# Depthwise filter matrices on 112 partitions, loaded by four transfers of 28 partitions each

## The chip, the cores and the metric

The kernel runs on one core of a Trainium2 chip. The metric is device time in microseconds (us) of one launch; less is better. Before the change, the median of three runs is 3448.89 us (3437.99 to 3469.41).

## The reference

Input `x` is 32 images of 384 channels, 28 x 28 pixels, all float32. Two layers follow each other.

```python
# layer 0: ConvNeXt block
y = conv(x, dw_w, padding 3, groups=384) + dw_b      # 7x7 depthwise
y = layernorm_over_channels(y) * ln_g + ln_b
y = gelu(einsum('bhwc,cf->bhwf', y, w1) + b1)        # 384 -> 1536
gx = sqrt(sum(y*y, axis=(h, w)))
y = grn_g * (y * gx / (mean_f(gx) + 1e-6)) + grn_b + y
x = x + einsum('bhwf,fc->bhwc', y, w2) + b2          # 1536 -> 384
# layer 1: gate
avg, mx, mn = mean, max, min of x over (h, w)
logits = concat(avg @ W1.T, grouped(mx, W2_1) * W2_2, mn @ W3.T) @ Wfc.T
out = sigmoid(logits[:, :, None, None] + x)
```

## The kernel before

The kernel has two stages. The first is the depthwise convolution of all images, channel by channel; the second takes image after image through the two channel matrix products (`up` and `down`), with a fast matrix scheme that needs sums of weight blocks. Those sums (`form_w`) are made by ScalarE and GpSimd during the first stage and stored in device memory (`u1d`, `u2d`). The change is in the first stage.

**How the convolution is tiled.** An image has 28 rows of 28 pixels. Four rows, 112 pixels, lie on 112 partitions (`RW = 4`, `HW = 28`, `KP = 112`), and the seven groups of four rows times 32 images are the 224 columns. For one channel, the convolution is a product with a banded matrix whose row for a pixel is the same sequence of filter taps, shifted. This sequence `fs` (355 values per channel, `FL`) is written once to device memory. The filter matrix of a channel is read out of it by a transfer whose source pattern overlaps itself: the partition for pixel row r and column w starts `r * PW + w` values further on (`PW = 32`). `load_t(s)` (L420 to L432) loads the matrices of eight channels (`TC = 8`) into one of four buffers `tmat`: each of 112 partitions gets 8 x 355 values, 11,360 bytes in one piece. Step 0 is loaded in two parts of four channels.

**A step.** There are 48 steps (`NK`), of eight channels each. A step has four calls of `conv`, two channels each. `conv` issues, per channel, three matrix products (L671, L673, L675; each float32 product shows as two MATMUL records) into a PSUM tile `pc`. VectorE then transposes `pc` into `yt` (L678) and adds it to the channel sum `acc` (L686), ScalarE squares it (L692), and GpSimd sums the squares (L698). At the end of a step, ScalarE's queue stores `yt` to device memory (`yd`, L837) and then the weight sums that are ready (L853). `yt` has two buffers, the weight sums `u` four.

**The images.** A block of 32 channels of all images comes as eight loads of `x` (L456, 392 KB each, into `room` and `xi_last`), is turned by TensorE (L477), and copied into `xt` by VectorE (L484) and ScalarE (L486). The turns of the next block are spread over the four steps of this one.

**Order.** Filters, `x` and weights are loaded from SyncE's queue (SP in the profile), in program order: at the start of step s, the filters of step s + 3 (L425); then weights or constants, if any (L785); then one x load after each turned block. A filter buffer is free when the step that used it last is through TensorE. The program gives transfers eight completion counters, in turn. `hold` (L601) makes the first filter loads wait for an x load.

The last two steps are done in two halves of 16 images, so that the statistics of the first half can be finished early; the loads of the first image and `first_image` follow.

Of the kernel before, what the change touches and what calls it, by code (L numbers as in the profile page):

```python
# [13 lines left out]
P = 128  # L14
# [4 lines left out]
HW = 28  # L19
# [10 lines left out]
RW = 4  # L30
NJ = HW // RW
PW = P // RW
KP = RW * HW
XC = 32
TC = 8
# [10 lines left out]
FL = S0 + SN  # L46
# [152 lines left out]
def convnext_gate_kernel(  # L199
# [13 lines left out]
    nc = tc.nc  # L213
# [149 lines left out]
    with ExitStack() as one:  # L363
# [40 lines left out]
        NT2 = 4  # L404
        tmat = [tp.tile([KP, TC, FL], F32, name=f"tmat_{i}") for i in range(NT2)]
# [15 lines left out]
        def load_t(s, parts=1):  # L421
            base = fs[s * TC // P]
            n = TC // parts
            for i in range(parts):
                nc.sync.dma_start(  # L425
                    tmat[s % NT2][:, i * n : (i + 1) * n, :].rearrange("p c m -> p (c m)"),
                    bass.AP(
                        tensor=base.tensor,
                        offset=base.offset + (s * TC % P + i * n) * FL,
                        ap=[[PW, RW], [1, HW], [1, n * FL]],  # L430
                    ),
                )  # L432


        NX = C // XC
# [170 lines left out]
        for i in range(NG):  # L606
            if i == 0:
                load_t(0, 2)
                nc.sync.dma_start(dwb, cvec[0:1, :].broadcast_to([P, C]))
            if i == NG - 2:  # L610
                for cb in range(CB):
                    if cb:
                        keep(sequences(cb))
                    keep(nc.scalar.dma_start(fs[cb][P:, :], zrow))
            if i == NG - 2:

                hold(tmat[1][:, 0, :1], i)
                load_t(1)
            for h in range(2):
                turn_x(i, h, xt, (nc.vector, nc.scalar)[h])  # L620
            load_next(i)
# [149 lines left out]
        for s in range(NK):  # L771
            k, si = divmod(s, SK)
            if s + 3 < NK:
                if s == 0:
                    for i in range(2, 4):
                        hold(tmat[i][:, 0, :1], NG)
                        if i == 2:
                            load_t(i)
                load_t(s + 3)
# [11 lines left out]
            if s == NK - 1:  # L791
# [6 lines left out]
                for half, (b0, b1) in enumerate(((0, B0), (B0, B))):  # L798
# [7 lines left out]
                    for n in range(2 * PAIRS):  # L806
                        i, c2 = divmod(n, PAIRS)
# [16 lines left out]
            elif s < NK - 2:  # L824
                for c2 in range(PAIRS):
# [5 lines left out]
                    elif q in (2 * PAIRS + 2, 2 * PAIRS + 5, 2 * PAIRS + 8):  # L831
                        n = FB + 4 * ((q - 2 * PAIRS) // 3)
# [455 lines left out]
```

## Time and profile before

| What | Value |
|---|---|
| Median of three runs | 3448.89 us |
| The profiled execution's own time | 3448.96 us |
| Its span in the profile | 3446.9 us |
| TensorE busy in the span | 3090.9 us (90%) |
| GpSimd / VectorE / ScalarE busy | 2432.2 / 1990.0 / 1736.7 us |
| Mean granted TensorE clock | 0.944 of full speed |
| First and last full-batch filter product (L671) | 30.7 and 880.3 us |
| Filter loads | 47 of 1242.5 KB, 2 of 621.2 KB |

The table of slices divides the span into 40 parts of 86 us; a digit is the busy share of an engine in tenths. DMA is the mean over the core's sixteen DMA engines, so a transfer that uses a few of them shows as a small share. "chain" is the sequence of work and waits, followed back from the last instruction. In the view by windows, a row is a stretch of time, the columns are the busy time of each engine, then granted clock, DMA share and GB/s. Lines of waits read: who waited, for what, us in total, how often, the longest.

### The profile page before, as it was taken

The numbers are of one execution on the slowest core, as the hardware profiler recorded it, in microseconds if no ns is written. First come the engines' busy times: TensorE is split into PE (matmuls) and PEld (weight loads), VectorE is DVE, ScalarE is ACT, GpSimd is POOL, SyncE is SP. The second block draws the span as 40 slices with busy tenths as digits, with TensorE's granted clock in tenths as the row PEclk, the third lists the DMA queues.
The fourth block names the chain that finished last, engine by engine and source line by source line (L and its number), as shares of the span: only waits on it lengthen the run. The fifth ranks groups of instructions, "written<-read, shape, count | busy, mean of one in ns | idle before, by whom it ended". The sixth has DMA issues, their size and how long they took to land.

```text
span 3446.9 us, 43986 instructions
## 1 busy us (share of the span) xinstructions
PE 3090.9 (90%) x14435; PEld 2498.4 (72%) x14435; DVE 1990.0 (58%) x4554; ACT 1736.7 (50%) x2916; POOL 2432.2 (71%) x1822
## 2 busy tenths in 40 slices
PE   6586665666799999999999999999999999999998
PEld 5476565565567777777778877777778887777788
DVE  2233232333666666666666666666666666666666
ACT  1122221222365666666655665666665666566662
POOL 1222244443579888887888888888888888888887
PEclk8778787778899999999999999999999999999999
DMA  5645555554645665655666666655666666655546
GB/s 181 190 172 181 182 202 182 187 179 162 214 130 179 219 204 192 195 192 193 206 199 200 211 216 204 193 194 190 194 207 201 200 214 208 209 193 190 190 156 197
DMA packets 287167, 664.51 MB, mean 193 GB/s; under 512 B 30675, under 2 KB 111086, under 8 KB 281678
## 3 DMA queue, kind: packets, MB, share of 16 engines
q1 hardware_dynamic: 253832, 569.28, 51.2%
q10 hardware_dynamic: 33110, 92.42, 7.0%
q8 instruction: 118, 1.93, 0.2%
q14 instruction: 107, 0.88, 0.1%
HBM read 566.85 MB, written 94.76 MB: 192 GB/s over the span
## 4 chain that ended last, share of the span: by engine, by line
PE 68%; DMA 22%; POOL 4%; DVE 3%; issue 1%; ACT 1%; SPq 0%; ACTq 0%; DVEq 0%; POOLq 0%
PE ph_C L941 12%; DMA tmat<-fs 11%; PE ph_A L941 10%; PE ph_B L941 10%; PE pz_A L1071 7%; PE pz_C L1071 7%; PE pz_F L1071 6%; PE pz_D L1071 6%; DMA room<-in_x 4%; PE pz_H L1071 2%; DMA u1d<-u 2%; PE pz_I L1071 2%; PE pz_E L1071 2%; POOL d_room L1032 1%; DVE room L316 1%; DMA ws<-in_w 1%
## 5 line engine op out<-in xcount | busy, mean ns | idle before, releaser
L327 ACT ACTIVATE y<-y,fv,gsc 128x784 f32<-128x784 f32 x372 | 359.1, 1030 | 464.5 <-DVE gsc L979 464.5
L1032 POOL TENSOR_TENSOR d_room<-y 128x588 f32<-128x588 f32 x253 | 364.4, 1441 | 289.0 <-PE pz_B L1071 192.2
L941 PE MATMUL ph_C<-room,ws 128*128 128x392 f32 x1240 | 462.4, 495 | 5.4 <-DVE y L956 2.9
L941 PE MATMUL ph_B<-room,ws 128*128 128x392 f32 x1240 | 460.2, 494 | 5.4 <-DVE room L359 5.4
L941 PE MATMUL ph_A<-room,ws 128*128 128x392 f32 x1240 | 459.0, 493 | 2.1 <-ACT te L948 1.7
L900 ACT ACTIVATE y<-y,b1f 128x784 f32<-128x784 f32 x384 | 350.3, 945 | 209.1 <-DVE y L958 179.0
L1032 POOL TENSOR_TENSOR d_room<-d_room,y 128x588 f32<-128x588 f32 x308 | 440.9, 1436 | 16.8
L671 PE MATMUL pc<-xt,tmat 112*128 112x224 f32 x736 | 236.4, 407 | 198.0 <-ACT sq L692 128.1
L678 DVE STREAM_TRANSPOSE yt<-pc 128x448 f32<-128x448 f32 x184 | 118.9, 646 | 473.9 <-PE pc L675 315.9
L941 PEld LDWEIGHTS ph_C<-room,ws 128*128 128x128 f32 x1240 | 233.7, 190 | 188.6 <-DVE y L956 28.7
L698 POOL TENSOR_TENSOR ssum<-ssum,sq 128x896 f32<-128x896 f32 (+1 forms) x100 | 200.7, 2007 | 235.7 <-ACT sq L692 233.6
L941 PEld LDWEIGHTS ph_A<-room,ws 128*128 128x128 f32 x1240 | 235.7, 190 | 175.1 <-ACT te L948 2.4
L941 PEld LDWEIGHTS ph_B<-room,ws 128*128 128x128 f32 x1240 | 235.5, 191 | 169.6 <-issue 5.8
L692 ACT ACTIVATE sq<-pc,dwb 128x224 f32<-128x224 f32 x368 | 141.4, 453 | 395.9 <-DVE acc L686 262.1
L913 ACT ACTIVATE junk<-y 128x784 f32<-128x784 f32 x384 | 329.0, 857 | 8.9
L1032 POOL TENSOR_TENSOR d_room<-y,d_room 128x588 f32<-128x588 f32 x214 | 306.1, 1436 | 27.2 <-PE pz_D L1071 15.8
L359 POOL TENSOR_TENSOR room<-room 128x392 f32<-128x392 f32 x303 | 303.5, 1018 | 11.9
L671 PEld LDWEIGHTS pc<-xt,tmat 112*128 112x128 f32 x736 | 143.0, 222 | 204.5 <-ACT sq L692 131.8
L1032 POOL TENSOR_TENSOR y<-y 128x588 f32<-128x588 f32 x180 | 258.8, 1438 | 7.1
L952 DVE TENSOR_TENSOR y<-y,ph_C 128x392 f32<-128x392 f32 x384 | 212.8, 562 | 24.9
L954 DVE TENSOR_TENSOR y<-y,ph_B 128x392 f32<-128x392 f32 x256 | 137.5, 557 | 153.0 <-ACT y L900 123.4
L673 PE MATMUL pc<-xt,tmat 112*96 112x192 f32 x736 | 205.2, 365 | 0.0
(261 smaller groups left out, 6443.0 us busy)
## 6 DMA issues: line engine op xcount, KB each, us to landing
u<-u2d SPq DMA_DIRECT2D x487, 384.0 KB
ws<-u1d SPq DMA_DIRECT2D x384, 320.0 KB
tmat<-fs SPq DMA_DIRECT2D x47, 1242.5 KB
ws<-u2d SPq DMA_DIRECT2D x121, 384.0 KB
yi<-yd SPq DMA_DIRECT2D x95, 448.0 KB
yd<-yt ACTq DMA_DIRECT2D x46, 896.0 KB
x<-in_x SPq DMA_DIRECT2D x32, 1176.0 KB
out<-x ACTq DMA_DIRECT2D x31, 1176.0 KB
```

The lines of the kernel that those rows point to most:

```text
L327: eng.activation(out, in_, AF.Identity, bias=add, scale=mul)
L359: tc.keep_in_program_order(eng.tensor_tensor(d, o[in0], o[in1], op))
L671: keep(nc.tensor.matmul(po, t[:, c, P : 2 * P], xc, start=True, stop=False))
L673: nc.tensor.matmul(lo, t[:, c, 2 * P : T0 + MW], after, start=False, stop=False)
L692: nc.scalar.activation(part(sq)[:, cy % SQ + ci], part(pc[:, :, :N])[:, ci], AF.Square, bias=dwb[:, cc + ci : cc + ci + 1], scale=1.0,)
L698: nc.gpsimd.tensor_tensor(part(ssum), part(ssum), part(sq), ALU.add)
L900: ins = nc.scalar.activation(y, y, AF.Gelu, bias=b1f[:, f : f + 1], scale=1.0)
L913: ins = nc.scalar.activation(junk, ys[b][:, f, :], AF.Square, accum_out=ssqs[b][:, f : f + 1])
L941: nc.tensor.matmul(banks[t, bk][:, :NH], wts[t][:, i % UG, :], o[opnd], start=(first == 1), stop=True, skip_group_check=True,)
L952: nc.vector.tensor_tensor(d, d, p, ALU.add)
L1032: nc.gpsimd.tensor_tensor(d[0], o[a][0], o[c][0], ALU.add if sign == "+" else ALU.subtract)
L1071: nc.tensor.matmul(pz[:, :NQ4], wt[:, i % UD, t, :], o[opnd][0][:, t, :], start=(first and t == 0), stop=(t == KD - 1), skip_group_check=True,
```

## The change

Each filter load becomes four transfers, one for each of the four pixel rows. A transfer writes 28 partitions, and its source pattern has 28 starting places one value apart, instead of 4 times 28. The bytes, their places, the buffers, and the order of everything else in the source are the same. The first load, which came in two parts, becomes eight transfers.

```diff
             for i in range(parts):
-                nc.sync.dma_start(
-                    tmat[s % NT2][:, i * n : (i + 1) * n, :].rearrange("p c m -> p (c m)"),
-                    bass.AP(
-                        tensor=base.tensor,
-                        offset=base.offset + (s * TC % P + i * n) * FL,
-                        ap=[[PW, RW], [1, HW], [1, n * FL]],
-                    ),
-                )
+                for r in range(RW):
+                    nc.sync.dma_start(
+                        tmat[s % NT2][r * HW : (r + 1) * HW, i * n : (i + 1) * n, :].rearrange(
+                            "p c m -> p (c m)"
+                        ),
+                        bass.AP(
+                            tensor=base.tensor,
+                            offset=base.offset + (s * TC % P + i * n) * FL + r * PW,
+                            ap=[[1, HW], [1, n * FL]],
+                        ),
+                    )
```

## The prediction, before the result was known

> **What bounds the kernel now.** I read the page first, for where the engines are not full.
>
> ```profile
> span 3446.9 us, 43986 instructions
> ...
> PE   6586665666799999999999999999999999999998
> ...
> PEclk8778787778899999999999999999999999999999
> DMA  5645555554645665655666666655666666655546
> ...
> PE 68%; DMA 22%; POOL 4%; DVE 3%; issue 1%; ACT 1%; SPq 0%; ACTq 0%; DVEq 0%; POOLq 0%
> PE ph_C L941 12%; DMA tmat<-fs 11%; PE ph_A L941 10%; PE ph_B L941 10%; PE pz_A L1071 7%; PE pz_C L1071 7%; PE pz_F L1071 6%; PE pz_D L1071 6%; DMA room<-in_x 4%; PE pz_H L1071 2%; DMA u1d<-u 2%; PE pz_I L1071 2%; PE pz_E L1071 2%; POOL d_room L1032 1%; DVE room L316 1%; DMA ws<-in_w 1%
> ```
>
> PE is full from slice 11 on; only the first ten or so slices (86 us each) have gaps, and a lower clock. DMA holds 22% of the chain, half of it the filter loads. So only the depthwise-convolution stage matters here. The filter line dates it, and the view by windows (columns as named; last three: granted PE clock, busy share of the 16 DMA engines, GB/s) shows its resources.
>
> ```profile
> L671 PE MATMUL pc<-xt,tmat x736: 351/353/743, 30.7 to 880.3; 112*128 112x224 f32 x184
> ```
>
> ```profile
> core 0: us, PE busy (x) PEld busy (x) DVE busy (x) ACT busy (x) POOL busy (x), PEclk, DMA share, GB/s
> 30.70:903.00 872.30, 572.36 (x3113) 535.29 (x3114) 284.48 (x513) 191.29 (x509) 299.33 (x209) 0.80 0.52 181
> 84.50:88.50 4.00, 4.00 (x27) 3.85 (x25) 0.00 (x0) 0.00 (x0) 0.00 (x0) 1.00 0.26 108
> 270.00:271.00 1.00, 1.00 (x9) 0.95 (x7) 0.78 (x2) 0.28 (x1) 1.00 (x1) 1.00 0.92 378
> 900.20:902.20 2.00, 2.00 (x21) 2.00 (x21) 1.93 (x3) 0.40 (x2) 1.14 (x1) 1.00 0.99 115
> ```
>
> No engine is full over the stage, DMA least of all at 0.52. The short windows say why it still binds. At 84.5 us only filter loads are in flight: share 0.26, 108 GB/s. That is four of sixteen engines, 27 GB/s each. The load's source pattern has 4 as its outermost count; the x loads, with 32 outermost, reach share 0.92 and 378 GB/s at 270 us (25.7 GB/s per engine).
>
> Work per engine in the stage, from the table of DMA issues: filters 47 x 1242.5 KB and 2 x 621.2 KB are 61.1 MB; over four engines at 27 GB/s that is 565 us. The rest (x 96 x 392 KB, yd 46 x 896 KB and 16 x 112 KB, u1d 15 x 256 KB, u2d 38 x 192 KB, weights 6 x 768 KB) is 98.7 MB; over sixteen at 25.7 that is 240 us. The four busy engines carry 805 us of a stage of 872. They are the bound, at 92%. The waits agree:
>
> ```profile
> SPq L456 <- DMA tmat<-fs: 242.2, 19, 17.8
> ```
>
> The x loads need nothing of the filters; they wait because the program gives eight completion counters out in turn, so that each transfer waits for the one eight before.
>
> **The change part by part.**
>
> *Added issues.* 49 transfers become 196. One costs SP 0.655 us (median of L425), so 147 x 0.655 = 96 us more on SP. A step (eight channels, one load) then has 4 x 0.655 for filters and 2 x 0.54 for x, 3.7 us of 10 or more: hidden behind PE and the transfers. Uncovered it would be 96 us. Behind these issues on SP stand the x loads, which run four steps ahead; the filters run three ahead.
>
> *The engines of one load.* 28 rows dealt to up to 16 engines leave two rows on the busiest, as 14 engines with two each would. At 27 GB/s each that is 378 GB/s, 3.4 us for a load's 1.27 MB, where four engines need 11.8 us. This is the good bound.
>
> *The rate of few partitions.* The window at 900.2 us has stores of 16 partitions alone: all engines busy (0.99), yet 115 GB/s instead of 378/0.92 = 411. Few partitions slow the engines that serve them. Scaled to 28 partitions it is 115 x 28/16 = 201 GB/s, and four quarters in a row take 6.3 us. Unscaled, 115 GB/s gives 11.1 us, the bad bound. I take 6.3, since 28 is nearer to 16 than to 128 and the slowdown followed the partition count there.
>
> [...]
>
> *The step after.* The other bytes cost 240/48 = 5.0 us of every engine per step. The busiest engine then has 3.4 + 5.0 = 8.4 us (good), 6.3 + 5.0 = 11.3 us (taken), 11.1 + 5.0 = 16.1 us (bad). The other limit is PE: in a stretch without stalls, at full clock, a step's first filter matmuls start at 263.08 and the next step's at 272.85, 9.8 us. DVE, ACT and POOL had 284, 191 and 299 us in the stage, 4 to 6.2 us per step, and follow. So DMA stays the bound by a little. Before, the stage ran 872/805 = 1.08 over its DMA work; I keep that: 12.2 us per step.
>
> *The counters.* About 8.4 transfers per step through eight counters: a step can't be shorter than 1.05 times the mean time from issue to landing. With 6 to 10 us for a landing it is covered by the step; what is late first if not is the yt store, whose two buffers leave it one step (DVE's yt L678 waits 125.7 us for it now).
>
> *The start.* ACT's turn of the last x block before the first convolution waits 16.1 us for the first filter load, behind a store that shares its counter. That load shrinks from 11.8 to 6.3 us or less: first convolution at about 24 instead of 30.7 us.
>
> *The sum.* 46 whole steps, then two half-batch steps from 880 to 903 us (23 us, with filters loaded before). 24 + 46 x 12.2 + 23 = 608 us for the end of the convolutions, against 903: 295 us gained. What follows (statistics, first images, the PE-bound rest) is untouched: the same instructions behind the same waits. The profiled execution took 3448.96 us (span 3446.9 and 2.1 outside), the median of the runs is 3448.89, so one serves for both: 3449 - 295 = 3154 us.
>
> **The rivals.**
>
> *PE takes over.* If quarters and other traffic interleave so that engines rarely meet on the same partitions, DMA needs 8.4 us and PE's 9.8 rules: 46 x 9.8 = 451, end at 24 + 451 + 23 = 498, 405 us gained, 3044 us; with the same 1.08 over, 10.6 us per step, 3081. For it: x loads and stores do mix in between. Against: 9.8 and 8.4 lie close, and each stall brings PE's clock down for some 4 us (0.50 from 284 to 288 us, 0.99 in the next window).
>
> *Few partitions cost the full price.* 115 GB/s: 16.1 x 1.08 = 17.4 us, end at 847, 56 us gained, 3393 us; halfway to the taken value 14.8 us, 3273. For it: the row is the only measured one. Against: 28 rows touch more than 16 do.
>
> *No gain.* If the four quarters ran strictly one after the other and each took a quarter of the present 11.8 us, nothing moves: 3449 us. It needs 108 GB/s for 28 partitions where 16 had 115. [...]
>
> *Slower: the counters decide.* If a 28-row transfer still ran on only the same four engines, eight counters would hold two filter loads instead of eight, and x loads and stores would queue behind quarters. The point is a mean landing of 18.5/1.05 = 17.6 us, the present step being (880.3 - 30.7)/46 = 18.5. The chain of waits has pieces of filter loads of 31 to 45 us now. At a mean of 20 us a step takes 21 us: 46 x 21 = 966, end at 1020 with the old start, 117 us lost, 3566 us.
>
> **How the numbers follow.** DMA bound at the taken price, 3100 to 3230 us: 0.52, the likeliest, 3154. PE bound, 3040 to 3100: 0.24. Full price of few partitions, 3230 to 3410: 0.15. No gain: 0.03. Slower: 0.06. The range 3050 to 3290 reaches into both neighbours and leaves out under 2 in 10. A change of 1% (34 us) is about what these runs can tell from none: faster 0.91, within it 0.03, slower 0.06.
>
> **What would show it.** Right: the first convolution near 24 us, the last near 608; DMA share over the stage 0.75 or more at 260 GB/s or so; no windows left with share 0.26; the wait of L456 for filter loads under 60 us; the same work after the stage at the same length. PE bound: share below 0.7 when no transfer is awaited, clock near 0.95. Wrong: filter loads still alone at 108 GB/s (engines not added), or high share at under 200 GB/s with steps of 16 us (partitions), or SP and ACT waiting on counters while the share is low.

## The result, and the profile after

The changed kernel takes 3223.04 us in the median of four runs (3199.34 to 3234.14), the kernel before 3443.44 us beside it (four runs, 3436.96 to 3469.41). The ratio is 0.934, with a 95% interval of 0.926 to 0.941. The forecast was 3154 us.

The profiled execution of the changed kernel is its fastest run: 3199.34 us, span 3197.5. Against the profiled execution before (span 3446.9) that is 249.4 us less, where the medians differ by 220. The reading below goes by the pair of profiles. From the page of the changed kernel (the span cut into 40 slices, now of 80 us; then the chain of work that ended last):

```profile
span 3197.5 us, 44190 instructions
...
PE   7698878889999999999999999999999999999998
...
PEclk9798988999999999999999999999999999999999
DMA  8879988875566666666566666666665666666645
...
PE 81%; DMA 8%; POOL 4%; DVE 4%; issue 1%; ACT 1%; SPq 1%; ACTq 0%; DVEq 0%; POOLq 0%
```

The row of DMA reads 7 to 9 in the first eight slices, where it read 4 to 6, and DMA's share of the chain fell from 22% to 8%. PE still has gaps, in eight slices instead of eleven. The filter line dates the stage, and the view by windows (busy time of each engine, then granted TensorE clock, busy share of the DMA engines, GB/s) shows its resources:

```profile
L674 PE MATMUL pc<-xt,tmat x736: 350/353/742, 18.6 to 637.6; 112*128 112x224 f32 x184
```

```profile
core 0: us, PE busy (x) PEld busy (x) DVE busy (x) ACT busy (x) POOL busy (x), PEclk, DMA share, GB/s
18.60:658.60 640.00, 536.54 (x3110) 507.31 (x3111) 290.66 (x517) 200.54 (x511) 299.90 (x209) 0.89 0.88 248
636.20:638.20 2.00, 2.00 (x14) 1.95 (x13) 1.40 (x3) 0.71 (x3) 1.52 (x1) 1.00 1.02 217
```

The stage from the first full-batch filter product to the last half-batch one shrinks from 872 to 640 us, at a DMA share of 0.88 instead of 0.52. The second row is a window in which almost only filter quarters are in flight: at a share of 1.02 they move 217 GB/s. The trace has 14 packets in flight there for most of the time, where with filter loads alone before (from 84.5 us) it has 4. With the earlier start, the convolutions end at 659 instead of 903 us. That is 244 of the 249 us; what follows takes 2538.5 instead of 2543.9 us.

The waits on SyncE's queue changed their kind:

```profile
SPq L426 <- DMA yd<-yt: 273.8, 31, 14.1
SPq L426 <- DMA tmat<-fs: 79.5, 51, 5.4
...
SPq L459 <- DMA tmat<-fs: 9.2, 6, 3.0
```

The x loads (now L459) wait for filter loads 9 us instead of 242. In their place the issues of filter quarters (now L426) wait 274 us for the stores of `yt`, in 31 long pieces. TensorE itself waits for filter loads 83 us, where it waited 30 us before:

```profile
PE pc L674 <- DMA tmat<-fs: 82.8, 25, 7.4
```

The chain of waits between 30 and 650 us (start, length, what) shows why some quarters are late. Eleven times a store on ScalarE's queue stands in it right before filter quarters, nine times of weight sums and twice of `yt`, 91 us of stores in all. One of them:

```profile
543.49 7.86 DMA u2d<-u
551.36 5.56 DMA tmat<-fs
```

A filter load needs nothing of such a store; by the program, only the completion counters that are given out in turn link the two.

### The profile page after: what moved, and what is told of

It is laid out like the page before. It is cut to its first block, busy times and chain, and to the rows that moved or that the text cites. A ratio compares the mean times of both kernels' runs of the same rounds, so it can differ in the third digit from the quotient of the medians.

```text
span 3197.5 us, 44190 instructions
## 1 busy us (share of the span) xinstructions
PE 3048.9 (95%) x14435; PEld 2465.1 (77%) x14435; DVE 1992.8 (62%) x4554; ACT 1745.3 (55%) x2916; POOL 2433.0 (76%) x1822
## 4 chain that ended last, share of the span: by engine, by line
PE 81%; DMA 8%; POOL 4%; DVE 4%; issue 1%; ACT 1%; SPq 1%; ACTq 0%; DVEq 0%; POOLq 0%
PE ph_C L944 13%; PE ph_A L944 11%; PE ph_B L944 11%; PE pz_A L1074 7%; PE pz_C L1074 7%; PE pz_F L1074 6%; PE pz_D L1074 6%; DMA tmat<-fs 4%; PE pc L674 3%; PE pc L676 3%; PE pc L678 3%; PE pz_H L1074 2%; PE pz_I L1074 2%; PE pz_E L1074 2%; DMA u2d<-u 2%; PE pt L480 1%
## 5 line engine op out<-in xcount | busy, mean ns | idle before, releaser
L327 ACT ACTIVATE y<-y,fv,gsc 128x784 f32<-128x784 f32 x372 | 359.1, 1030 | 463.6 <-DVE gsc L982 463.6
L674 PE MATMUL pc<-xt,tmat 112*128 112x224 f32 x736 | 222.2, 386 | 91.8 <-DMA tmat<-fs 82.8
L674 PEld LDWEIGHTS pc<-xt,tmat 112*128 112x128 f32 x736 | 133.5, 208 | 99.0 <-issue 70.8
L1074 PE MATMUL pz_A<-d_room,u 128*128 128x196 f32 x1050 | 202.8, 329 | 0.1
```

The costliest lines, as they stand in the source:

```text
L327: eng.activation(out, in_, AF.Identity, bias=add, scale=mul)
L674: keep(nc.tensor.matmul(po, t[:, c, P : 2 * P], xc, start=True, stop=False))
L1074: nc.tensor.matmul(pz[:, :NQ4], wt[:, i % UD, t, :], o[opnd][0][:, t, :], start=(first and t == 0), stop=(t == KD - 1), skip_group_check=True,
```

## The experiments

A *step* below is the time from the first to the last full-batch filter product, divided by 46: 18.5 us before, 13.5 us after. Three theories were to be told apart. *A*: the DMA engines are the bound; what matters is how many engines one load uses, and the rate at which few partitions take data. *B* and *C*: the number of transfers matters, since eight completion counters let only eight be under way; the quarters use them up, and so the loads look less far ahead. The diffs show the main lines of each edit.

### More transfers without more engines: bychannel

The kernel before, with each load cut by channels instead of by rows. All the parts keep the old source pattern.

```diff
-                load_t(s + 3)
+                load_t(s + 3, 4)
```

> As before, with the pattern that uses four engines, but each filter load split into four transfers of two channels each, all on 112 partitions. It adds the transfers of the change without its engines. Theory A: the same four engines carry the same bytes, 3430 to 3480 us, as before. Theory B (counters; the prediction's slower rival): the eight counters hold two loads instead of eight, x loads and stores queue behind them, 3500 to 3570 us.

It took 3464.0 us, ratio 1.004 (1.0015 to 1.007), step 18.8 us. As many transfers as the change has, but 4 rows outermost as before, cost 0.4% and gain nothing. The window over most of its stage is nearly that of before (0.52 and 181 GB/s from 60 to 860 us):

```profile
60.00:860.00 800.00, 504.62 (x2674) 470.55 (x2672) 248.15 (x437) 159.43 (x433) 259.06 (x177) 0.78 0.52 177
```

So the gain doesn't come from shorter transfers, and the crowding of the counters costs little where the engines are the bound.

### More engines without more transfers: single

One transfer again, with the two counts of the source pattern exchanged, so that 28 is outermost. The pixels land in another order on the partitions of `tmat`, while those of `xt` stay where they are, so other pixels are convolved.

```diff
-                        ap=[[PW, RW], [1, HW], [1, n * FL]],
+                        ap=[[1, HW], [PW, RW], [1, n * FL]],
```

> One transfer per filter load as before, but with 28 as the outermost count of its source pattern (pixel column outermost, pixel row inner), so that it should use 14 engines over all 112 partitions. (The pixels of xt are left where they were, as in spread; the times stay.) Theory A: close to spread, 3080 to 3140 us; a little slower if neighbouring engines meet on the same partitions. Theory B, counters: 49 transfers instead of 196, so that the wait of SP's filter line for yt stores falls under 60 us, and faster than after as well, 3060 to 3120 us. So single alone does not separate them; if spread stays at after's time and single gains, it is the counters. If the outermost count does not set the engines, 3440 us as before.

It took 3121.2 us, ratio 0.904 (0.898 to 0.909), step 11.6 us:

```profile
60.00:530.00 470.00, 423.57 (x2558) 404.73 (x2557) 238.75 (x422) 162.40 (x423) 255.49 (x175) 0.94 0.93 290
```

The same bytes in the same number of transfers as before gain 9.6%; only the outermost count of the source differs. Filter loads alone had a share of 0.26 before, four packets in flight, and the stage's share rises from 0.52 to 0.93 here: the engine count of one load was the bound. It also gains 100 us more than the change does: with loads that spread over 112 partitions the stage moves 290 GB/s at a share of 0.93, where with quarters on 28 partitions it moved 248 at 0.88. How much of that is the partitions, the next run shows.

### The same four transfers, spread over all partitions: spread

Transfer r writes partitions r, r + 4, and so on (other pixels again, as in *single*).

```diff
-                        tmat[s % NT2][r * HW : (r + 1) * HW, i * n : (i + 1) * n, :].rearrange(
+                        tmat[s % NT2][r::RW, i * n : (i + 1) * n, :].rearrange(
```

> As after, with four transfers of 28 rows per filter load in the same order, but transfer r writes partitions r, r+4, r+8 ... instead of 28 neighbours, so each spans all 112 partitions. (The pixels of xt are left where they were, so the convolution mixes other pixels; shapes, counts and times of the work stay.) Theory A, few neighbouring partitions slow the engines that serve them: in after a filter row of 11,360 bytes runs at half rate; spread, it returns to nearly full rate, the filters cost an engine about 3.5 us of a step instead of 6, PE becomes the bound at 9.8 to 11 us a step instead of 13.5, the last convolution starts near 520 to 560 us instead of 658, and the time is 3080 to 3130 us. Theory B, the eight completion counters hold the filter transfers up (SP's filter line waits 274 us for yt stores in after): counts and order are the same, so the step stays at 13.5 us and the time at 3200 to 3235 us.

It took 3164.3 us, ratio 0.918 (0.912 to 0.924), step 12.7 us, between the two forecasts. The window and the first wait of SyncE's queue:

```profile
60.00:570.00 510.00, 435.32 (x2542) 412.69 (x2541) 239.93 (x415) 165.09 (x418) 252.37 (x173) 0.92 0.80 263
```

```profile
SPq L426 <- DMA yd<-yt: 252.6, 32, 14.0
```

More bytes (263 GB/s) at a lower share (0.80): per unit of share 263/0.80 = 329 GB/s, against 248/0.88 = 282 after the change. So the rate of 28 neighbouring partitions does cost engine time. But the step fell by 0.8 us only, and the engines are no longer full: most of what remains is not the partitions' rate. The queue waits nearly as long for `yt` stores as after the change (253 and 274 us), and TensorE still waits for filter loads, where in *single* it waits 0.7 us:

```profile
PE pc L674 <- DMA tmat<-fs: 64.6, 27, 5.6
```

In the chain between 60 and 570 us, stores of `yt` hold 21.7%, mostly with a filter quarter right behind; in *single* (60 to 530 us) they hold 5.0%. So both theories have a part here: the partitions' rate, and loads that are issued late, behind a store (the counter as the link is read from the program, not tested).

### Fewer partitions still: sixteen

The quarters of the changed kernel are cut once more, into 16 and 12 rows.

```diff
+                    for w0, w1 in ((0, 16), (16, HW)):
```

> As after, but each 28-row transfer split into one of 16 and one of 12 rows, eight transfers per load; 16 and 12 engines then serve 16 and 12 partitions. Theory A with the prediction's law (rate follows the number of neighbouring partitions, 115 GB/s at 16): a filter row takes about four times 426 ns, some 1500 ns or more, a load 11 to 13 us, the step 16 to 19 us, 3340 to 3470 us. If engines counted and partitions did not: as after or better, 3150 to 3220 us. Theory C alone: as the run eight, 3218 us.

One run: 3466.5 us, beside 3449.2 for the kernel before; step 18.5 us. The whole stage, and a window with almost only filter loads:

```profile
60.00:860.00 800.00, 539.87 (x2744) 502.46 (x2744) 257.93 (x448) 179.49 (x454) 271.44 (x185) 0.79 0.85 179
871.40:873.40 2.00, 2.00 (x13) 1.95 (x13) 1.34 (x4) 0.78 (x2) 0.72 (x1) 1.00 1.13 91
```

The whole gain is gone, at a DMA share of 0.85. How many engines served the parts of 12 rows, no view shows. This is the price of few partitions at its plainest: filter loads alone get 217 GB/s on 28 partitions and 91 on 16 and 12. It also doubles the number of transfers, which the next run does by itself.

### Twice the transfers, same partitions: eight

Every load of the changed kernel is cut by channels into two parts, so it has eight transfers of 28 partitions.

```diff
-                load_t(s + 3)
+                load_t(s + 3, 2)
```

> As after, but every filter load in two parts of four channels, so eight transfers of 28 partitions with half the bytes each. Theory A (rate of few partitions): same bytes through the same engines and partitions, step 13.5 to 14 us, 3210 to 3250 us. Theory B (counters): 12.4 transfers per step instead of 8.4 through eight counters, step up to 13.5 x 12.4/8.4 = 19.9 us, 3350 to 3520 us.

It took 3218.0 us, ratio 0.932 (0.927 to 0.937), step 13.4 us: no change against 3223. Eight transfers fill all counters by themselves, and the look-ahead in transfers is halved; the forecast of that theory, 3350 us and more, fell. So *sixteen* lost its gain to the partitions, not to the number of its transfers. The number isn't the whole of theory B, though: SyncE's loads of filters and x still wait 258 us for `yt` stores, and TensorE 75 us for filters.

### Half the transfers: wide

Two neighbouring filter buffers become one, and four transfers load 16 channels, at every second step.

```diff
-                load_t(s + 3)
+                load_pair(s + 2)
```

> The 28-row transfers of after, but each over sixteen channels, for two steps at once, into two buffers of sixteen channels instead of four of eight: two filter transfers per step instead of four, same bytes, rows and partitions. Theory C: SP's look-ahead is back at two steps, the wait for yt stores falls from 274 us to under 100, the step falls from 13.5 to 12 to 12.6 us (what is left is the engines' work, 6.1 us of filter rows and 6.2 of the rest), 3145 to 3185 us. Theory A alone: rates unchanged, step 13.5, 3200 to 3235 us.

It took 3203.3 us, ratio 0.927 (0.923 to 0.931), step 13.1 us. Time and step are nearer to what theory A forecast alone. Half the transfers gain 0.3 us per step, near the limit of what can be told; but a double buffer also comes free only when both of its steps are through, so the edit changes more than the number. The queue still waits 182 us for `yt` stores (two lines, 134 and 48). A later run joins *spread* and *wide*:

> wide and spread together: transfers of 28 rows over sixteen channels, two per step, each over partitions r, r+4, r+8 ... (the pixels of xt stay where they were). Two limits lie side by side by now: the engines' time with neighbouring partitions (left alone in wide, step 13.1 us at a DMA share of 0.93) and the wait of SP's filter loads for yt stores through the counters (left alone in spread, step 12.7 us at a share of 0.80). If that is so, with both taken away the step falls to 11 to 11.8 us, near single's 11.6, and the time to 3085 to 3135 us, with SP waiting under 100 us for yt stores. If spread's step was set by something else, this stays at 12.5 to 13 us, 3150 to 3185 us.

*spreadwide* took 3162.9 us, ratio 0.915 (0.910 to 0.920): no better than *spread* with 3164.3. The time lies in the second range of the forecast, but its step (12.1 us) lies between the two, so neither case holds as written. The shorter step doesn't show in the time, since its half-batch end took 37 instead of 20 us (see the last section). SyncE still waits 187 us for `yt` stores on two lines, and TensorE 25 us for filter loads.

### One transfer against four, 28 rows outermost: single4

*single*, with each load cut by channels into four.

```diff
-                load_t(s + 3)
+                load_t(s + 3, 4)
```

> The pattern of single (28 outermost, all 112 partitions, 14 engines), but each filter load as four transfers of two channels. Bytes, engines and partitions per load are those of single; the transfers per step are those of after (8.4). (As in single, the pixels of xt stay where they were.) Theory C, look-ahead in transfers: with eight counters in turn, SP can run only eight transfers past a yt store that has not landed; four transfers per load make that one step instead of two, so the last quarter of a load is issued some 5 us before its step instead of 30, and a step is the landing of a yt store plus that of a quarter. Then single4 loses most of what single gained over spread: step 12.3 to 13 us, 3150 to 3185 us, SP's filter line waiting 200 us or more for yt stores. Theory A alone (rates of few partitions): as single, 11.6 us a step, 3110 to 3130 us.

It took 3100.6 us, ratio 0.899 (0.894 to 0.904), step 11.0 us:

```profile
60.00:510.00 450.00, 416.69 (x2579) 398.83 (x2578) 238.67 (x422) 161.47 (x427) 258.77 (x177) 0.96 0.97 307
```

It has as many transfers as the change, yet its median lies 21 us below that of *single* (their ranges overlap: 3094.99 to 3117.26 and 3107.71 to 3122.35), and its filter issues wait only 3.5 us for `yt` stores. So the number of transfers through eight counters doesn't by itself hold the change back; it matters when they are issued. A part of two channels needs only the two channels it overwrites to be done, so it can be issued earlier than a quarter, which holds all eight; that this is the reason was argued from the code and not tried by itself.

### Whole kernels on this path: turned, turned2, turned4, turned5

To use *single* in a kernel that computes the reference, the pixels of `xt` must follow. ScalarE copies each block of x from row order into column order before it is turned:

```diff
+                nc.scalar.activation(
+                    xw.rearrange("p (j w r) -> p j w r", w=HW, r=RW),
+                    xis[i].rearrange("p (j r w) -> p j w r", w=HW, r=RW),
+                    AF.Identity,
+                )
```

> single made whole: the filter load is one transfer with pixel column outermost, and ScalarE copies each block of x into the order column, row before TensorE turns it (96 copies of 128 x 784, about 0.9 us each, 1.8 us of ScalarE per step, on top of 4 us). If that stays hidden: as single plus some 5 to 10 us at the start, 3120 to 3145 us. If ScalarE's copies delay its squares and the stores behind them: 3150 to 3200 us.

*turned* took 3188.9 us, ratio 0.922 (0.918 to 0.927), step 12.5 us. A copy takes 1.57 us, not the 0.9 expected, and with a single buffer TensorE waits for it 74 times, 114 us:

```profile
PE pt L489 <- ACT xw L472: 114.3, 74, 18.4
```

*turned2* has two copy buffers, at the price of one x buffer, and copies a block ahead; *turned4* adds the parts by channel of *single4*; *turned5* gives every second copy to VectorE.

```diff
+            if i % 2:
+                keep(nc.scalar.activation(dst, src, AF.Identity))
+            else:
+                keep(nc.vector.tensor_copy(dst, src))
```

> turned with two buffers for the reordered x block and the copy one block ahead (the ring of x blocks has seven places instead of eight to make room). In turned, TensorE waited some 110 us for these copies (96 of 1.57 us). With the copy ahead this wait goes, the step falls from 12.5 to 11.5 us as in single, 3120 to 3150 us. If ScalarE's 3.1 us more per step is what delays, 3170 to 3190 us.

> turned2 with each filter load in four transfers of two channels, as in single4, so that a part can be loaded as soon as its two channels are done. If single4's 20 us against single carry over: 3095 to 3130 us. If ScalarE sets the pace, as turned2.

> turned4 with every second reordering copy on VectorE instead of ScalarE. In turned4 ScalarE spends 3.2 us of a step on these copies and TensorE waits 45 us for them in the stage. If they delay the step, halving ScalarE's part brings 11.2 us down to 10.7 to 11 us, 10 to 25 us in all: 3105 to 3125 us. If VectorE, which every convolution passes through, is delayed as much: 3125 to 3145 us.

| Kernel | us | ratio (95%) | step, us |
|---|---|---|---|
| turned2 | 3177.0 | 0.920 (0.915 to 0.925) | 12.5 |
| turned4 | 3130.0 | 0.906 (0.901 to 0.910) | 11.3 |
| turned5 | 3115.0 | 0.903 (0.898 to 0.908) | 11.3 |

*turned2* missed the time forecast for its edit. It lies in the second range, but *turned4* has the same copies on ScalarE and a step of 11.3 us, so ScalarE's work isn't what sets the step. TensorE still waits 85 us for copies, and SyncE's x loads 201 us (174 in *turned*); the shorter ring may add to that, which was not tried by itself. The parts by channel are what helped. *turned4* and *turned5* have the same step; their profiles differ by the half-batch end, 37 against 20 us, so it isn't shown that moving copies to VectorE gains anything else, and that *turned5* lies in its forecast range is luck. *turned5* is the best kernel that computes the whole reference: 108 us (3.4%) below the changed kernel, of which up to 17 us may be the half-batch end. The runs of the kernel before beside it scattered more than elsewhere, from 3436.84 to 3505.16 us.

## Why the prediction was right, and where it was off

**The bound of the kernel before: right.** *single* and *bychannel* separate what the argument had joined. Four engines carried the filters (a share of 0.26 with filter loads alone); one transfer with 28 outermost, at a stage share of 0.93, gains 9.6%, more transfers with 4 outermost, at 0.52, nothing. The rival "no gain" fell: the split by partitions gained 6.6%. But the better way was to keep one transfer and reorder its pattern.

**The price of few partitions: right.** 201 GB/s for the filters was scaled from a row of 16-partition stores; the window of filter loads alone shows 217. That one row carried the whole scaling. The full price (115 GB/s) didn't come. *sixteen* shows that the price is real: 91 GB/s and the loss of the whole gain. In the packets of the traces a filter row of 11,360 bytes took 426 ns in the median before and 820 ns after.

**The other bytes of a step: mis-sized.** One term that was off is the 5.0 us per step for x, stores and weights, their bytes at the best rate seen (25.7 GB/s per engine, from 270 to 271 us). The prediction read that window as x loads; in it 0.29 of 0.38 MB went through ScalarE's queue, which had issued a store of `yt` at 269.03 us. The stage's own share gives more. Before, 0.52 x 16 engines x 872.3 us = 7258 engine-us were busy; the filters' 61.1 MB at 27 GB/s take 2263 of them, and 4995/16/48 = 6.5 us per step are left for the rest. This is a remainder: it takes the filters at 27 GB/s also beside other traffic, which no view shows by itself. The stores alone were near the price (from 60 to 500 us 25.04 MB at a share of 0.152, 23 GB/s per engine), so most of the missing time lies with what SyncE's queue loads. After, 0.88 x 16 x 640 = 9011; less 4995 that is 4016 for the filters, and over 14 engines (as in the prediction; the trace has 14 packets in flight from 636.2 us) and 48 loads 6.0 us each (6.3 forecast). So a step has 6.0 + 6.5 = 12.5 us of work instead of 11.3; 13.46 us was measured, again 1.08 over the work. The forecast had 12.2; in 46 steps the difference is 58 us. The 6.5 could be worked out from the window that the prediction quotes. It also changes what the 1.08 means: with it the four engines carried 565 + 48 x 6.5 = 877 us in a stage of 872, so by this estimate they were simply full, and the 1.08 of before was the missing work of the other bytes. The 1.08 of after is another thing: engines that are not full, with issues that wait for stores. That the old factor fits it is luck.

**The start and the end: nearly right.** The first convolution starts at 18.6 us (24 forecast), 5 us better. The two half-batch steps took 21 us (23 assumed), and the rest of the kernel 5 us less. So 3154 - 5 + 58 - 2 - 5 = 3200, beside 3199.34 of the profiled execution. The median lies 24 us above that. Only one execution of the changed kernel was profiled, so where these 24 us went stays open; the half-batch end described below costs 17 us when it runs at half clock, which would be most of them. The mean clocks on record fit that: 0.977 in the profiled execution, 0.970 to 0.972 in the other three, and with the end at half clock 0.977 would become 0.971 by my estimate (20.5 us at 1.00 turned into 37.7 at 0.50). It is argued and not shown.

**The counters: put at nothing, and not nothing.** "Covered by the step" priced these waits at zero; this step of the argument failed. The filter quarters wait 274 us for `yt` stores, the store that the prediction named as late first, and eleven stores, 91 us together, stand right before filter quarters in the chain. So a part of the 58 us above probably comes from this wait; how they divide between bytes and waits is not shown. The number of transfers isn't the reason: *eight* doubles them without a change, *wide* halves them for 0.3 us, and *single4* has as many without these waits. The rival of a slower kernel priced at 3566 us would have shown in *bychannel*, which keeps four engines and took 3464.

**The added issues: hidden.** 147 more issues at 0.655 us were to be covered. *eight* adds 188 more and is not slower.

**The signs.** First convolution 18.6 us (24 forecast), end of the convolutions 659 (608), share 0.88 (0.75 or more), 248 GB/s (260), L459's wait for filters 9 us (under 60), the rest of the kernel 2538.5 us (2543.9 before). No window with filter loads alone at 0.26 is left: of the 4 us windows from 20 to 656 us the lowest has a share of 0.28, without a packet of 8 KB or more, and a filter row has 11,360 bytes. TensorE did not become the bound: it was busy 536.5 of the 640 us at a clock of 0.89.

**What stays open.** The steps of *spread* and *spreadwide* (12.7 and 12.1 us at shares of 0.80 and 0.89) are longer than that of *single* (11.6), whose bytes and partitions are the same. The traces say where the time goes: TensorE waits 65 and 25 us for filter loads there, and 0.7 us in *single*, and in *spread* the late loads stand behind stores of `yt`. *single4* excludes the number of transfers by itself. But no run gives the filter loads counters of their own or changes the order of the quarters against the stores, so what these waits cost, after the change too, is read from chains and not tested.

## What to carry to other kernels

Read the DMA share of a window in which only one kind of transfer is in flight: a low share there (0.26 here, four packets in flight) named a transfer that used few engines, where the mean share of the stage was 0.52. Then try to make a count outermost that spreads one transfer over many engines and many partitions before cutting it into pieces: at a share of about one, pieces on 28 neighbouring partitions moved 217 GB/s here, and pieces on 16 and 12 moved 91. To price what shares the engines, take the busy share of the stage itself times its length, not bytes over the best rate of a short window, and see which queue moved the bytes of that window. Then look in the chain for transfers that stand behind others that they don't need.

## What the runs showed of the hardware that was not expected

**A busy DMA engine is no measure of bytes.** The share adds up the whole times of the packets that start in a window, so that it can pass one (1.02 and 1.13 here). At a share of about one, the engines moved 378 GB/s (mostly a store of `yt`, at 0.92, from 128 partitions), 217 (28 partitions at a time) and 91 (16 and 12). *sixteen* has a share of 0.85 over its stage and moves 179 GB/s, where the kernel before moved 181 with 0.52.

**The half-batch end at half clock.** The last two steps are the same instructions in the changed kernel and in *wide*. In the profile of the one they ran at full clock, in the other at half, with TensorE busy all the time:

```profile
638.50:659.00 20.50, 20.12 (x192) 19.99 (x192) 16.86 (x39) 8.94 (x31) 12.16 (x11) 1.00 0.90 261
```

```profile
629.30:667.00 37.70, 37.70 (x189) 37.70 (x190) 16.51 (x39) 9.22 (x32) 16.78 (x14) 0.50 0.49 142
```

The first row is the changed kernel, the second *wide*: 17 us apart. Of the profiles, before, after, *spread*, *single*, *single4*, *bychannel* and *turned5* have the short form, *eight*, *wide*, *sixteen*, *spreadwide*, *turned*, *turned2* and *turned4* the long one, all at a clock of 0.50 or 0.51. What decides it was not found; the pause before it doesn't, since from the last full-batch product to the first half-batch one 1.9 us pass in *turned4* (long) as in *turned5* (short); up to 17 us of a difference between two of these profiles may be this and not the edit.

**A copy that reorders pixels costs more.** 128 x 784 values with a step of 28 between neighbours took 1.57 us on ScalarE and 1.52 us on VectorE. In the kernel before, ScalarE's passes over 128 x 784 values in their order took 0.86 us (L913) to 1.03 us (L327).
